# Attention scores of both kinds issued alternately, and a new body for the overflow branch

## The chip, the cores and the metric

The kernel runs on one core of a Trainium2 chip. The metric is the device time of one execution in microseconds; the median of several runs is given. The engines of a core are called PE (TensorE, the matrix engine; PEld are its weight loads), DVE (VectorE), ACT (ScalarE), POOL (GpSimd) and SP (SyncE). Each has its own queue of instructions and waits on semaphores for the others.

## The reference

The input is x of 16 sequences of 256 tokens with 256 features. With xn = layernorm(x), the result is x + attention(xn) + experts(xn).

```python
qkv = einsum('bsd,ed->bse', xn, w_qkv) + b_qkv          # 16 heads of 16
q, k = rotated q and k
scores = einsum('bhqd,bhkd->bhqk', q, k) / sqrt(16)      # causal
attn = softmax(scores); out = einsum('bhqk,bhkd->bhqd', attn, v)

probs = softmax(xn @ router_w.T)                         # 8 experts
w = probs, kept up to a cumulated share of 0.9, else 0
out = sum over e of (silu(xn @ gate_w[e].T) * (xn @ up_w[e].T)) @ down_w[e].T * w[:, e]
```

There are 4096 tokens. An expert works only on the tokens whose weight for it is not zero. Everything is float32.

## The kernel before

**Attention.** A sequence is worked in 8 steps (b, c, p): c is one of 4 chunks of four heads and p one half of a chunk, so a step is two heads (j = 0, 1). Each head's 16 features are padded to 32 rows of the array; a step uses rows 64p to 64p+63. Two kinds of score products exist. `scores` (line 531, tile `s`) has queries on the partitions: a product of 128 columns for the first 128 queries (line 537) and one of 256 for the others (line 543), for both heads. After them `maxima` (line 549) adds the causal mask by a bf16 product (line 552), and DVE takes the row maxima (line 558). When all 8 steps of a sequence are through, `turn` (line 564) adds the negative maxima to the queries as a further feature. `probabilities` (line 577, tile `st`) then computes the same scores with keys on the partitions: 256 columns (line 583), 128 columns (line 589), the mask (line 595), and ACT takes the exponential (line 600). `weigh` multiplies by the values (line 610), `finish` turns the result and adds it to x.

A loop over 128 steps (line 675) issues, in each turn, the scores of step i, the probabilities of step i - 11 (`LAG`, an odd number, so the two kinds use different halves of the array's rows), the maxima of step i, and pieces of the next sequence's preparation and of the router. Each `s` and each `st` tile takes two PSUM banks, one a head, from a pool of three (`ps_sc`, line 239). A scheduler lays out the queue of each engine; in it the four products of s stand ahead of the four of st, or, in some steps, the 128-column pair of s stands ahead of other work and the 256-column pair just ahead of st.

**Experts.** Each expert has room for 1472 tokens (`CAP`) in 12 blocks, and one expert with too many may use one block more. POOL gathers the tokens' rows by indirect DMA (line 362), PE multiplies (lines 755 and 796), and POOL adds the weighted result into the output by an indirect DMA (`contract`, line 802).

**The overflow branch.** If more tokens are without a slot, a flag (`overflow`, read at line 851) sends all engines into a branch (line 854) that goes over all experts: it places the tokens past the slots block by block, gathers their rows, computes and scatters. With these inputs the flag is 0 and the branch is not taken. Its instructions are part of the program, and the engines jump past them; on the way round, the DMA semaphores are raised to the values which they would have after the branch, so that the waits at the end of the program (shown as line 925) hold for both ways.

Of the kernel before, what the change touches and what calls it, by code (L numbers as in the profile page):

```python
# [30 lines left out]
def kernel(  # L31
# [356 lines left out]
    with tc.tile_pool(name="prep", bufs=2) as prep, tc.tile_pool(  # L388
# [139 lines left out]

        W = 3 * P

        def scores(b, c, p):

            qT, kT, _, _ = seqs[b]
            sc = ps_sc.tile([P, 2, 512], F32, tag="sc", name=f"s_{b}_{c}_{p}")
            for j in range(2):
                rows = slice(32 * (2 * p + j), 32 * (2 * p + j) + 32)
                nc.tensor.matmul(  # L537
                    sc[:, j, :P], qT[rows, c, :P], kT[rows, c, :P],
                    start=True, stop=False, skip_group_check=True,
                )  # L540
            for j in range(2):
                rows = slice(32 * (2 * p + j), 32 * (2 * p + j) + 32)
                nc.tensor.matmul(  # L543
                    sc[:, j, P:W], qT[rows, c, P:], kT[rows, c, :],
                    start=False, stop=False, skip_group_check=True,
                )
            return sc

        def maxima(b, c, p, sc):
            for j in range(2):  # L550
                for k in (0, 2):
                    nc.tensor.matmul(  # L552
                        sc[:, j, ts(k, P)], ident_h, mask_h,
                        start=False, stop=True, skip_group_check=True,
                    )
            for qi in range(NQ):
                lo, hi = (0, P) if qi == 0 else (P, W)
                ins = nc.vector.tensor_reduce(  # L558
                    top[b % 2][:, qi, 2 * p : 2 * p + 2, HD + c], sc[:, :, lo:hi],
                    AX.X, ALU.max, negate=True,  # L560
                )
            return ins
# [11 lines left out]
            for c in range(CH):  # L574
                nc.gpsimd.tensor_tensor(qT[:, c, :], qT[:, c, :], topT, ALU.add)  # L575

        def probabilities(b, c, p):

            qT, kT, _, _ = seqs[b]
            sc = ps_sc.tile([P, 2, 512], F32, tag="sc", name=f"st_{b}_{c}_{p}")  # L580
            for j in range(2):
                rows = slice(32 * (2 * p + j), 32 * (2 * p + j) + 32)
                nc.tensor.matmul(  # L583
                    sc[:, j, : 2 * P], kT[rows, c, :P], qT[rows, c, :],
                    start=True, stop=False, skip_group_check=True,
                )
            for j in range(2):
                rows = slice(32 * (2 * p + j), 32 * (2 * p + j) + 32)
                nc.tensor.matmul(
                    sc[:, j, 2 * P : W], kT[rows, c, P:], qT[rows, c, P:],  # L590
                    start=False, stop=False, skip_group_check=True,
                )
            for j in range(2):
                for k in (0, 2):
                    nc.tensor.matmul(  # L595
                        sc[:, j, ts(k, P)], ident_h, maskT_h,
                        start=False, stop=True, skip_group_check=True,
                    )
            pr = probs.tile([P, 2, W], F32, tag="pr", name=f"pr_{b}_{c}_{p}", bufs=6)
            nc.scalar.activation(pr, sc[:, :, :W], AF.Exp)  # L600
            return pr
# [73 lines left out]
        for i in range(len(steps) + LAG + 5):  # L675
            if i < len(steps):
                b, c, p = steps[i]
                if i % PPS == 0 and b + 1 < B:
                    if b > 0:
                        open_seq(b + 1)  # L680
                    jobs = prep_seq(b + 1, turns_only=b == 0)
                sc = scores(b, c, p)
            if 0 <= i - LAG < len(steps):
                k = i - LAG
                prs[k] = probabilities(*steps[k])
            if i < len(steps):
                behind = maxima(b, c, p, sc)
                if jobs is not None:
                    job = next(jobs, None)
                    if job is not None:  # L690
                        job()
                with tc.issue_after(behind.ins):
                    if stat_next < NT:
                        sums_of(stat_next)
                        stat_next += 1
                    if i in stat_jobs:
                        statistics(*stat_jobs[i])

                if i == 2 * PPS + PPS // 2:
                    with tc.issue_after(stored[3].ins):  # L700
                        load_expert(0)
                if i == 3 * PPS:
                    with tc.issue_after(sums[4 * NQ - 1].ins):
                        zero_fill()


                if i % PPS == 5 and b % 2 == 0 and b + 1 < B:
                    parts = router(b * NQ, 2 * NQ)
                    todo = [lambda parts=parts: next(parts, None)] * 6
                    if b + 2 == B:  # L710
                        todo += [
                            lambda: count(0),
                            lambda: find_wave(0, 0),
                            lambda: fetched.update({0: fetch(*work[0])}),
                            lambda: find_wave(0, 1),
                            lambda: fetched.update({1: fetch(*work[1])}),
                        ]
                for _ in range(1 if b + 2 < B else 2):
                    if todo:
                        todo.pop(0)()  # L720
            k = i - 1
            if 0 <= k < len(steps) and k % PPS == PPS - 1:
                turn(steps[k][0])
            k = i - LAG - 2
            if 0 <= k < len(steps) and k % 2 == 1:
                held[k] = weigh(steps[k][0], steps[k][1], (prs.pop(k - 1), prs.pop(k)))
            k = i - LAG - 3
            if 0 <= k < len(steps) and k % 2 == 1:
                finish(steps[k][0], steps[k][1], held.pop(k))


    with tc.tile_pool(name="hid", bufs=2) as hid:
# [55 lines left out]

        added = {}

        def contract(e, k, hT, xg, token, n, name, alone=False):

            _, _, d_sb = expert_w[e]
            py = ps_m.tile([P, D], F32, tag="m", name=f"py_{name}_{k}")
            for i in range(IC):
                nc.tensor.matmul(  # L796
                    py[:n, :], hT[:, i, k * P : k * P + n], d_sb[:, i, :],
                    start=(i == 0), stop=(i == IC - 1),
                )
            ys = hid.tile([P, D], F32, tag="ys", name=f"ys_{name}_{k}", bufs=6)  # L800
            nc.scalar.activation(ys[:n, :], py[:n, :], AF.Copy, scale=weights_of(e, xg, n))  # L801
            ins = nc.gpsimd.indirect_dma_start(  # L802
                out=out, out_offset=bass.IndirectOffsetOnAxis(ap=token, axis=0),
                in_=ys[:n, :], in_offset=None, compute_op=ALU.add,
            )

            if not alone:
                for other in added.setdefault(e, []):
                    tc.declare_no_dep(ins.ins, other, reason="no token in common")
                added[e].append(ins.ins)  # L810

        xT, hT = {}, {}

# [38 lines left out]
            overflow, min_val=0, max_val=1, skip_runtime_bounds_check_because="0 or 1"  # L852
        )
        with tc.If(many > 0):
            upper = gat.tile([P, P], F32, tag="upper", name="upper", bufs=1)
            own = gat.tile([P, 1], F32, tag="own", name="own", bufs=1)
            more = gat.tile([P, P], F32, tag="more", name="more", bufs=1)
            four = gat.tile([P, 4, 1], I32, tag="four", name="four", bufs=1)
            for e in range(E):
                load_expert(e)  # L860
                nc.vector.tensor_scalar(upper, slot[:, :P], float(CAP), None, ALU.add)
                nc.vector.tensor_scalar(own, mine[:, 0:1], float(CAP), None, ALU.add)
                with tc.For_i(0, -(-(NT * P - CAP) // P), 1):
                    place_slots(e // 4, upper, more)
                    nc.vector.tensor_scalar(upper, upper, float(P), None, ALU.add)
                    find(e // 4, (0,), more, own, four, f"o{e}")
                    nc.vector.tensor_scalar(own, own, float(P), None, ALU.add)
                    token = four[:, e % 4, :]
                    xg = fetch_block(token, f"o{e}")
                    xo = open_in(f"o{e}")  # L870
                    turn_in(xo, 0, xg, f"o{e}")
                    ho = open_hidden(f"o{e}")
                    for q in range(IC):
                        expand(e, q, xo, ho, P, f"o{e}")
                    contract(e, 0, ho, xg, token, P, f"o{e}", alone=True)


# [51 lines left out]
```

## Time and profile before

| what | value |
|---|---|
| median of 3 runs | 1006.89 us (1004.35, 1006.89, 1007.24) |
| profiled execution | 1005.13 us, of which the span from first to last instruction is 1002.9 us |
| mean granted clock of TensorE | 0.983 |
| 40 to 440 us (attention) | PE busy 380.6 of 400 us |
| 440 to 520 us (its end, the first experts) | PE busy 78.4 of 80 us |
| 520 to 985 us (experts) | PE busy 463.9 of 465 us |
| 985 to 1003 us (end) | PE busy 0.5 of 18 us |

Busy times of PE are modelled and the products are pipelined, so a busy PE does not mean that it works at its peak; a wait shorter than a product's length can hide in it. The page of the profile gives engine shares and the costliest lines; the timeline gives single instructions in order of time; a query by source line also lists sequencer instructions (waits, branches, drains), marked by a q behind the engine's name (POOLq, SPq).

### The profile page before, as it was taken

The numbers are of one execution on the slowest core, as the hardware profiler recorded it, in microseconds if no ns is written. First come the engines' busy times: TensorE is split into PE (matmuls) and PEld (weight loads), VectorE is DVE, ScalarE is ACT, GpSimd is POOL, SyncE is SP. The second block draws the span as 40 slices with busy tenths as digits, with TensorE's granted clock in tenths as the row PEclk, the third lists the DMA queues.
The fourth block names the chain that finished last, engine by engine and source line by source line (L and its number), as shares of the span: only waits on it lengthen the run. The fifth ranks groups of instructions, "written<-read, shape, count | busy, mean of one in ns | idle before, by whom it ended". The sixth has DMA issues, their size and how long they took to land. (4 is left out here: it accounts for less than half of the span.)

```text
span 1002.9 us, 17633 instructions
## 1 busy us (share of the span) xinstructions
PE 955.6 (95%) x7076; PEld 666.2 (66%) x7076; DVE 428.2 (43%) x1268; ACT 316.7 (32%) x617; POOL 393.5 (39%) x473
## 2 busy tenths in 40 slices
PE   7999999999999999899999999999999999999993
PEld 3576667676767676675676666766766667666672
DVE  6777665757575756725111234332211111111210
ACT  3444644443444344252222221212222222222220
POOL 6324223232222222423455454444444545547332
PEclk9899999999999999899999999999999999999997
DMA  7124100000020000101243343242432524324221
GB/s 237 29 80 151 38 23 23 18 23 24 22 86 23 2 23 2 37 30 53 43 89 69 50 93 62 43 111 43 96 70 44 115 49 96 65 48 98 40 27 22
DMA packets 46362, 57.54 MB, mean 57 GB/s; under 512 B 9312, under 2 KB 37600, under 8 KB 46272
## 3 DMA queue, kind: packets, MB, share of 16 engines
q0 software_dynamic: 19360, 29.81, 16.7%
q1 hardware_dynamic: 26912, 26.52, 8.4%
q8 instruction: 58, 0.95, 0.4%
q14 instruction: 32, 0.26, 0.1%
HBM read 32.14 MB, written 24.17 MB: 56 GB/s over the span
## 5 line engine op out<-in xcount | busy, mean ns | idle before, releaser
L802 POOL DMA_INDIRECT out<-ys,tokens x96 | 152.0, 1583 | 239.6 <-ACT ys L801 186.3
L761 DVE TENSOR_TENSOR hT<-act,gu 128x384 f32<-128x384 f32 (+2 forms) x132 | 70.0, 530 | 333.2 <-ACT act L760 328.5
L755 PE MATMUL gu<-xT,wg 128*128 128x384 f32 (+1 forms) x512 | 182.7, 479 | 1.4 <-DVE hT L761 1.0
L796 PE MATMUL py<-wd,hT 128*128 128x256 f32 (+1 forms) x768 | 182.4, 380 | 0.0
L755 PE MATMUL gu<-xT,wu 128*128 128x384 f32 (+1 forms) x512 | 179.5, 473 | 0.0
L558 DVE TENSOR_REDUCE top<-s 128x2 f32<-128x256 f32 (+1 forms) x256 | 131.0, 552 | 100.3 <-PE s L552 100.3
L796 PEld LDWEIGHTS py<-wd,hT 128*128 128x128 f32 (+1 forms) x768 | 141.5, 186 | 41.7 <-issue 3.8
L760 ACT ACTIVATE act<-gu 128x384 f32<-128x384 f32 (+2 forms) x132 | 62.3, 472 | 285.0 <-PE gu L755 280.5
L600 ACT ACTIVATE pr<-st 128x768 f32<-128x768 f32 x128 | 103.7, 810 | 127.1 <-PE st L595 121.6
L755 PEld LDWEIGHTS gu<-xT,wu 128*128 128x128 f32 x512 | 97.6, 191 | 61.5 <-issue 0.9
L755 PEld LDWEIGHTS gu<-xT,wg 128*128 128x128 f32 x512 | 89.8, 191 | 40.9 <-DVE hT L761 2.7
L362 POOL DMA_INDIRECT xg<-rows,tokens x96 | 94.6, 985 | 40.3 <-issue 20.7
L583 PE MATMUL st<-qT,kT 32*128 32x256 f32 x512 | 90.7, 430 | 1.8 <-DVE less L328 1.0
L631 POOL TENSOR_TENSOR xs<-xs,at 128x128 f32<-128x128 f32 x64 | 29.2, 456 | 145.2 <-DVE at L627 144.7
L801 ACT ACTIVATE ys<-py,xg 128x256 f32<-128x256 f32 x96 | 45.5, 474 | 120.9 <-PE py L796 114.7
L543 PE MATMUL s<-kT,qT 32*128 32x256 f32 x512 | 81.9, 391 | 1.0
L467 POOL TENSOR_TENSOR qp<-qk,rot 128x256 f32<-128x256 f32 x32 | 23.3, 729 | 121.9 <-DVE qk L466 121.9
L610 PE MATMUL o<-pr,va 128*32 128x256 f32 (+1 forms) x1024 | 56.8, 336 | 13.7 <-DVE at L627 11.6
L439 PE MATMUL pq<-wqkv_sb,xnT 128*128 128x512 f32 x128 | 65.4, 635 | 0.2
L537 PE MATMUL s<-kT,qT 32*128 32x128 f32 x512 | 63.4, 322 | 1.1 <-DVE top L558 0.8
L575 POOL TENSOR_TENSOR qT<-qT,topT 128x256 f32<-128x256 f32 x64 | 45.2, 738 | 41.0 <-ACT topT L573 41.0
L537 PEld LDWEIGHTS s<-kT,qT 32*128 32x128 f32 x512 | 39.0, 184 | 23.8 <-issue 21.2
(161 smaller groups left out, 1140.2 us busy)
## 6 DMA issues: line engine op xcount, KB each, us to landing
rows<-xn SPq DMA_DIRECT2D x32, 128.0 KB, 1.8
wg<-in_wg SPq DMA_DIRECT2D x8, 512.0 KB, 3.7
wu<-in_wu SPq DMA_DIRECT2D x8, 512.0 KB, 4.7
wd<-in_wd SPq DMA_DIRECT2D x8, 512.0 KB
out<-xs SPq DMA_DIRECT2D x16, 256.0 KB, 2.1
xs<-in_x SPq DMA_DIRECT2D x3, 1024.0 KB, 9.5
rows<-zeros POOLq DMA_DIRECT2D x1, 1716.0 KB
out<-zeros POOLq DMA_DIRECT2D x1, 1664.0 KB
```

The costliest lines, as they stand in the source:

```text
L362: nc.gpsimd.indirect_dma_start(out=xg[:n, :], out_offset=None, in_=rows, in_offset=bass.IndirectOffsetOnAxis(ap=token, axis=0),)
L439: nc.tensor.matmul(pq, xnT[:, c, ts(qi, P)], wqkv_sb[:, c, : 2 * D], start=(c == 0), stop=(c == DC - 1),)
L537: nc.tensor.matmul(sc[:, j, :P], qT[rows, c, :P], kT[rows, c, :P], start=True, stop=False, skip_group_check=True,)
L543: nc.tensor.matmul(sc[:, j, P:W], qT[rows, c, P:], kT[rows, c, :], start=False, stop=False, skip_group_check=True,)
L558: ins = nc.vector.tensor_reduce(top[b % 2][:, qi, 2 * p : 2 * p + 2, HD + c], sc[:, :, lo:hi], AX.X, ALU.max, negate=True,)
L583: nc.tensor.matmul(sc[:, j, : 2 * P], kT[rows, c, :P], qT[rows, c, :], start=True, stop=False, skip_group_check=True,)
L600: nc.scalar.activation(pr, sc[:, :, :W], AF.Exp)
L755: nc.tensor.matmul(gu[:, j, :w], w_sb[:, c, ts(i, P)], xT[:, c, :w], start=(c == 0), stop=(c == DC - 1),)
L760: nc.scalar.activation(act[:, :w], gu[:, 0, :w], AF.Silu)
L761: nc.vector.tensor_tensor(hT[:, i, :w], act[:, :w], gu[:, 1, :w], ALU.mult)
L796: nc.tensor.matmul(py[:n, :], hT[:, i, k * P : k * P + n], d_sb[:, i, :], start=(i == 0), stop=(i == IC - 1),)
L802: ins = nc.gpsimd.indirect_dma_start(out=out, out_offset=bass.IndirectOffsetOnAxis(ap=token, axis=0), in_=ys[:n, :], in_offset=None, compu ...
```

## The change

`scores` and `probabilities` no longer issue their products. A new function `products` is given the step of the scores and the step of the probabilities, takes a tile for each, and issues first the 128-column pairs of both, then the 256-column pairs of both. For st the 128-column pair is now the one that starts its PSUM bank. The masks, maxima and exponentials follow in the order as before.

The overflow branch gets a new body. It sets the weights of tokens that have a slot to zero, writes the weights back to the table, and then every expert goes over all 32 token tiles with plain DMAs from SP: load the rows, compute, load the output, add on DVE, store. `contract` is split: `product` ends with the weighted result, and `contract` adds the scatter.

```diff
-        def scores(b, c, p):
...
-        def probabilities(b, c, p):
...
+        def products(now, late):
+            made = []
+            for step, by_key in ((now, False), (late, True)):
+                if step is None:
+                    made.append(None)
+                    continue
+                b, c, p = step
+                qT, kT, _, _ = seqs[b]
+                sc = ps_sc.tile(
+                    [P, 2, 512], F32, tag="sc", name=f"{'st' if by_key else 's'}_{b}_{c}_{p}"
                 )
+                made.append((kT if by_key else qT, qT if by_key else kT, c, p, sc, by_key))
+            for first in (True, False):
+                for left, right, c, p, sc, by_key in filter(None, made):
+                    if by_key:
+                        to, lhs = (slice(2 * P, W), slice(P, S)) if first else (
+                            slice(0, 2 * P), slice(0, P))
+                    else:
+                        to, lhs = (slice(0, P),) * 2 if first else (slice(P, W), slice(P, S))
+                    for j in range(2):
+                        rows = slice(32 * (2 * p + j), 32 * (2 * p + j) + 32)
+                        nc.tensor.matmul(
+                            sc[:, j, to], left[rows, c, lhs],
+                            right[rows, c, lhs if first else slice(0, S)],
+                            start=first, stop=False, skip_group_check=True,
+                        )
+            return [m and m[4] for m in made]
...
-                sc = scores(b, c, p)
-            if 0 <= i - LAG < len(steps):
-                k = i - LAG
-                prs[k] = probabilities(*steps[k])
+            k = i - LAG
+            sc, scT = products(
+                steps[i] if i < len(steps) else None,
+                steps[k] if 0 <= k < len(steps) else None,
+            )
+            if scT is not None:
+                prs[k] = probabilities(*steps[k], scT)
...
         with tc.If(many > 0):
-            upper = gat.tile([P, P], F32, tag="upper", name="upper", bufs=1)
...
+            for h in range(NH):
+                place_of = ps_m.tile([P, P], F32, tag="m", name=f"place_{h}")
+                nc.tensor.transpose(place_of, order[h][:, :P], ident)
...
+            nc.sync.dma_start(rt[:, :, D:], wts)
             for e in range(E):
                 load_expert(e)
...
-                    token = four[:, e % 4, :]
-                    xg = fetch_block(token, f"o{e}")
+                with tc.For_i(0, NT, 1) as t:
+                    tile_rows = bass.ts(t, P)
+                    xg = gat.tile([P, D + E], F32, tag="xg", name=f"xg_o{e}")
+                    nc.sync.dma_start(xg, rows[tile_rows, :])
...
-                    contract(e, 0, ho, xg, token, P, f"o{e}", alone=True)
+                    ys = product(e, 0, ho, xg, P, f"o{e}")
+                    had = hid.tile([P, D], F32, tag="had", name=f"had_o{e}", bufs=1)
+                    nc.sync.dma_start(had, out[tile_rows, :])
+                    nc.vector.tensor_tensor(had, had, ys, ALU.add)
+                    nc.sync.dma_start(out[tile_rows, :], had)
```

More of the change, by code (lines that the diff above doesn't have):

```diff
@@ L529 @@
         W = 3 * P
-        def scores(b, c, p):
[L533 to L539, printed above, removed]
-                )
[L541 to L547, printed above, removed]
+        def products(now, late):
[8 more added lines that the diff above has]
+                    [P, 2, 512], F32, tag="sc", name=f"{'st' if by_key else 's'}_{b}_{c}_{p}"
+                )
+                made.append((kT if by_key else qT, qT if by_key else kT, c, p, sc, by_key))
[14 more added lines that the diff above has]
+            return [m and m[4] for m in made]
         def maxima(b, c, p, sc):
@@ L575, in turn, with probabilities @@
                 nc.gpsimd.tensor_tensor(qT[:, c, :], qT[:, c, :], topT, ALU.add)
-        def probabilities(b, c, p):
[L579 to L592, printed above, removed]
+        def probabilities(b, c, p, sc):
             for j in range(2):
@@ L789, with product @@
         added = {}
-        def contract(e, k, hT, xg, token, n, name, alone=False):
+        def product(e, k, hT, xg, n, name):
             _, _, d_sb = expert_w[e]
@@ L801, in contract @@
             nc.scalar.activation(ys[:n, :], py[:n, :], AF.Copy, scale=weights_of(e, xg, n))
+            return ys
+        def contract(e, k, hT, xg, token, n, name):
+            ys = product(e, k, hT, xg, n, name)
             ins = nc.gpsimd.indirect_dma_start(
@@ L805, in contract @@
             )
[L807 to L810, printed above, removed]
+            for other in added.setdefault(e, []):
+                tc.declare_no_dep(ins.ins, other, reason="no token in common")
+            added[e].append(ins.ins)
         xT, hT = {}, {}
@@ L854 @@
         with tc.If(many > 0):
-            upper = gat.tile([P, P], F32, tag="upper", name="upper", bufs=1)
-            own = gat.tile([P, 1], F32, tag="own", name="own", bufs=1)
-            more = gat.tile([P, P], F32, tag="more", name="more", bufs=1)
-            four = gat.tile([P, 4, 1], I32, tag="four", name="four", bufs=1)
+            for h in range(NH):
+                place_of = ps_m.tile([P, P], F32, tag="m", name=f"place_{h}")
+                nc.tensor.transpose(place_of, order[h][:, :P], ident)
+                es = slice(4 * h, 4 * h + 4)
+                nc.vector.scalar_tensor_tensor(
+                    wts[:, :, es].rearrange("p t e -> p e t"),
+                    place_of.rearrange("p (e t) -> p e t", e=4), float(CAP),
+                    wts[:, :, es].rearrange("p t e -> p e t"), ALU.is_gt, ALU.mult,
+                )
+            nc.sync.dma_start(rt[:, :, D:], wts)
             for e in range(E):
                 load_expert(e)
[L861 to L867, printed above, removed]
-                    token = four[:, e % 4, :]
-                    xg = fetch_block(token, f"o{e}")
+                with tc.For_i(0, NT, 1) as t:
+                    tile_rows = bass.ts(t, P)
+                    xg = gat.tile([P, D + E], F32, tag="xg", name=f"xg_o{e}")
+                    nc.sync.dma_start(xg, rows[tile_rows, :])
                     xo = open_in(f"o{e}")
```

## The prediction

> **What bounds the kernel.** I read the page first, then TensorE's timeline around the score products, then the last 20 us by source line.
>
> ```profile
> span 1002.9 us, 17633 instructions
> ...
> PE 955.6 (95%) x7076; PEld 666.2 (66%) x7076; DVE 428.2 (43%) x1268; ACT 316.7 (32%) x617; POOL 393.5 (39%) x473
> ```
>
> TensorE is busy for 95% of the span and every other engine for under half. So a change in the order of TensorE's products counts nearly one for one, and the rest counts only where TensorE has nothing left: at the end. A typical attention step in the timeline of PE (start, length, line, output and inputs, count; an f32 product of two heads shows as two pairs of passes):
>
> ```profile
> 207.74 0.38 PE L537 MATMUL s<-kT,qT 32*128 32x128 f32 x2
> 207.76 0.48 PE L583 MATMUL st<-qT,kT 32*128 32x256 f32 x2
> 207.95 0.28 PE L537 MATMUL s<-kT,qT 32*128 32x128 f32 x2
> 208.06 0.38 PE L543 MATMUL s<-kT,qT 32*128 32x256 f32 x2
> 208.09 0.38 PE L583 MATMUL st<-qT,kT 32*128 32x256 f32 x2
> 208.28 0.38 PE L543 MATMUL s<-kT,qT 32*128 32x256 f32 x2
> 208.30 0.39 PE L589 MATMUL st<-qT,kT 32*128 32x128 f32 x4
> 208.62 0.40 PE L595 MATMUL st<-maskT_h,ident_h 128*128 128x128 bf16 x4
> ```
>
> This is the main finding. In program order all s products stand before st, yet st starts 27 ns after s (unrounded starts), before the second s pass. The two kinds, on different rows of the array, already run side by side. From the first s to the mask product is 0.88 us, and st's own part, 207.76 to 208.62, is what ends last. In other steps st waits for its PSUM tile, and s goes on alone meanwhile:
>
> ```profile
> 320.72 0.38 PE L537 MATMUL s<-kT,qT 32*128 32x128 f32 x2
> 320.80 0.48 PE L583 MATMUL st<-qT,kT 32*128 32x256 f32 x2
> 320.93 0.28 PE L537 MATMUL s<-kT,qT 32*128 32x128 f32 x2
> ...
> 321.66 0.40 PE L595 MATMUL st<-maskT_h,ident_h 128*128 128x128 bf16 x4
> ```
>
> Here st starts 86 ns after s, and again needs 0.854 us to the mask. In a third kind of step other products stand between the 128- and the 256-column s, and the latter starts just ahead of st. The end of the kernel, by source line (engine, operation, count, ns min/median/max, first and last start):
>
> ```profile
> L854 POOLq EVENT_SEMAPHORE  x4: 17/43/1592, 990.6 to 992.4; - x4
> ...
> L854 POOLq COMPARE_BRANCH  x1: 53/53/53, 987.7 to 987.7; - x1
> ...
> L854 POOLq INC_SWDGE_SEM  x1: 2022/2022/2022, 992.5 to 992.5; - x1
> ```
>
> ```profile
> L925 SPq EVENT_SEMAPHORE  x14: 17/28/28, 994.4 to 1002.8; - x14
> L925 POOLq EVENT_SEMAPHORE  x4: 17/17/17, 1002.1 to 1002.8; - x4
> L925 POOLq DRAIN  x3: 50/113/7541, 994.5 to 1002.6; - x3
> ```
>
> The branch is not taken. On its way past it POOL waits for the last scatter to land (the 1592 ns wait, until 992.3), then raises eight DMA semaphores for 2.02 us, and only then begins a drain of 7.54 us (994.5 to 1002.07). The closing barrier takes the last 0.84 us. All of this lies at the end of the span with nothing beside it; that the page's chain of waits stops at 988.9 hides it.
>
> **What the Trainium skill says.** "TensorE: Matmul & The Clock Gate", section The mechanism (packing by rows), says products on different row groups run concurrently, but also that products are in strict order of the program. The trace agrees with the first and not with the second: st passes s products that stand ahead of it. "Runtime: NRT & Kernel Launch", section Instruction fetch mechanics, says a taken branch outside the fetched window waits for its page; POOL's 2.9 us from branch (987.7) to next instruction (990.6) agrees. "VectorE: DVE Perf Modes", section The DRAIN you can't avoid, calls closing drains about 12 ns, constant on all engines; SP, ACT and DVE show 7 to 17 ns here, but POOL shows 7541.
>
> **The change, part by part.** In the compiled order of the two kernels, ahead of the branch DVE, ACT, POOL and SP have the same instructions with the same waits. On TensorE only the score products move: st's 128-column pair goes ahead of s's 256-column pair, and st's 256-column pair comes last. Counts and sizes are equal.
>
> (1) Steps like 207.74. st now has two products ahead of it instead of four; at 27 ns for four it starts about 13 ns after s. Its order becomes 128 then 256, as s has today. s's chain runs from 207.739 to its last pass at 208.282 plus one 256-column pass (213 ns: the two first st starts are 320 apart, less a 107 ns weight load): 756 ns. st's chain is 645 ns to its last start plus a 107 ns pass: 752 ns. So the new st chain should be 4 ns longer, then the same 102 ns until the mask. Net: 13.5 - 4 = 9 ns saved. Sorting all steps by the offset of st to s gives 47 such steps: 0.44 us.
> (2) Steps of the third kind, 27: the 256-column s is no longer ahead of st; 14 ns saved, 4 lost: 0.27 us.
> (3) Steps in which st waits, 43: the wait is for ScalarE's exponential of the step before, and ends when it did. Now s's 256-column pair is queued behind it. Released together with st's, it needs about 550 ns (load plus two passes), under st's 756: hidden. If the passes did not overlap it would cost 2 x 213 ns a step. I take the 4 ns: 0.17 us lost. The 11 steps with st alone lose 0.04 us.
> The sum for TensorE is 0.44 + 0.27 - 0.17 - 0.04 = 0.5 us saved; bounds 0.5 us lost (no gain at the start, 4 ns on all 128) to 1.7 us saved (13.5 ns on all).
>
> (4) The branch's body is not executed in either kernel. But its new body issues no DMA from POOL, and so the way round it changes: the four POOL waits and the raising of semaphores are gone from it; after its jump POOL comes straight to the drain. SP now waits for the last scatter itself, some 0.85 us of waits after 992.3, so until 993.1. POOL's fetch after the branch (2.9 us) stays, so the drain starts at about 990.7 instead of 994.53: 3.85 us earlier. What is late next is the drain itself. Its length without the raising ahead of it is shown nowhere. If it goes with the 204 DMAs that POOL issued (97 gathers, 97 scatters, 8 weight gathers, 2 fills; 7541 / 204 = 37 ns each, my estimate), it is unchanged: the drain ends at 998.2, and 3.85 us are saved. Lower bound of the gain: nothing, if the drain takes over all that was done ahead of it. Upper: 8.9 us, if without the raising it is nearly empty; then SP's waits (993.1) and the 0.84 us barrier close the kernel at 994.0. I take 3.85 because the count of DMAs is the same.
>
> Sum: 0.5 + 3.85 = 4.35 us off the profiled execution of 1005.13 us (span 1002.9, 2.2 outside it): 1000.8 us. The three timed runs (1004.35, 1006.89, 1007.24) lie around it with a median 1.8 higher, so I put the forecast between 1000.8 and 1006.89 - 4.35 = 1002.5: 1001.8 us, which takes 1006.15 as the kernel before. The cases below are counted from there.
>
> **The rivals.** A: the forecast, 1001.8, chance 0.50. 0.3% (3 us) is what a measurement of this kernel can tell from no change, so it counts mostly as faster.
> B: the drain gets short too: 0.5 + 8.9 = 9.4 us saved, 996.7 us. For it: the other drains are 0.05 to 0.18 us, and the long one stands right after the raising. Against: it would have to be caused by an instruction that the profile already charges 2.02 us. Chance 0.15.
> C: the drain waits for the last landing before its work, or takes over half of what was ahead: 992.3 + 7.5 ends at 999.8, so 2.3 + 0.5 = 2.8 us saved or less: 1003.4 to 1004.5. For it: the wait for the landing stood ahead of the drain so far. Against: SP now waits for it too. Chance 0.17.
> D: the end doesn't move, and the TensorE gain of 0.5 us can't be seen: the change does not do what its words say, since the two kinds already ran side by side: 1005.6. For it: nothing in the trace of before tells the drain's length from its end. Chance 0.11.
> E, slower: with st's short pair between s's two pairs, the products no longer pass each other, and s's 256-column load starts only after st's second 128-column pass, 110 ns late, in 117 steps: 12.9 us lost, less 3.85 at the end: 1015.2. It decides from 59 ns a step (117 x 59 = 6.9 us, the 3.85 and 0.3%). Against it: at 207.95 and 208.06 the trace shows s products starting as soon as their own rows are free. Chance 0.07.
>
> **How the numbers follow.** The range may leave out 0.2: it reaches from 996.3 (most of B) to 1006.5 (C, and D with a scatter of 1 us), and leaves out E and the low end of B. Faster by over 0.3%: most of A (0.42), all of B (0.15), a quarter of C (0.04): 0.61. Slower: 0.06 of E and 0.01 of D: 0.07. The rest, 0.32, is the same.
>
> **What would show it.** In the timeline of the changed kernel, st's first pass 13 ns after s, the mask 0.87 us after the first s (0.88 before), and 0.86 after st in steps in which st waits; a mask more than 0.95 after s speaks for E. At the end: no POOLq INC_SWDGE_SEM at the branch, and a long POOLq DRAIN that starts about 3.4 us after the last scatter (987.35 before) and lasts 7.5 us (A), under 2 us (B), or 9 to 11 us (C, D). The prediction is wrong if the drain's end doesn't move, or if SP's waits get late.

## The result

The changed kernel takes 995.04 us (median of 12 runs, 993.16 to 1002.84), the kernel before 1005.14 us (median of 12 runs, 1000.17 to 1010.04). The ratio is 0.9907, with a 95% interval from 0.9881 to 0.9934: faster, by 6.6 to 12 us. The forecast was 1001.8 us with a range down to 996.3. The sign is right; the gain of the medians, 10.1 us, is 2.3 times the 4.35 us forecast, and the time lies outside the range.

The profiled execution of the changed kernel took 994.29 us. Head of its page, as shown for the kernel before:

```profile
span 992.5 us, 17632 instructions
...
PE 946.2 (95%) x7076; PEld 636.7 (64%) x7076; DVE 428.3 (43%) x1268; ACT 316.8 (32%) x617; POOL 393.2 (40%) x473
```

The same number of products and of weight loads; PE is busy for 9.4 us less, while the span is 10.4 us shorter. So most of the gain lies in time in which PE counted as busy. A typical step in PE's timeline of the changed kernel (start, length, line, output and inputs, count):

```profile
399.68 0.38 PE L556 MATMUL s<-kT,qT 32*128 32x128 f32 x2
399.69 0.38 PE L556 MATMUL st<-qT,kT 32*128 32x128 f32 x2
399.89 0.28 PE L556 MATMUL s<-kT,qT 32*128 32x128 f32 x2
399.91 0.28 PE L556 MATMUL st<-qT,kT 32*128 32x128 f32 x2
400.01 0.38 PE L556 MATMUL s<-kT,qT 32*128 32x256 f32 x2
...
400.24 0.38 PE L556 MATMUL st<-qT,kT 32*128 32x256 f32 x2
400.55 0.40 PE L596 MATMUL st<-maskT_h,ident_h 128*128 128x128 bf16 x4
```

st starts 13 ns after s (27 before), the mask stands 870 ns after the first s (881 before). This is what was predicted, and it is small. The gain is elsewhere. One step in eight is the first of a new sequence. PE and then ScalarE around such a step, in the kernel before:

```profile
404.56 0.38 PE L622 MATMUL ot<-ident,oT 128*128 128x128 f32 x2
404.87 0.49 PE L537 MATMUL s<-kT,qT 32*128 32x128 f32 x4
405.43 0.48 PE L543 MATMUL s<-kT,qT 32*128 32x256 f32 x2
405.45 0.48 PE L583 MATMUL st<-qT,kT 32*128 32x256 f32 x2
...
405.98 0.39 PE L589 MATMUL st<-qT,kT 32*128 32x128 f32 x4
406.30 0.40 PE L595 MATMUL st<-maskT_h,ident_h 128*128 128x128 bf16 x4
```

```profile
404.80 0.58 ACT L483 COPY qT<-qt 128x512 f32<-128x512 f32 x1
```

and the same step in the changed kernel:

```profile
401.76 0.38 PE L556 MATMUL s<-kT,qT 32*128 32x128 f32 x2
401.85 0.38 PE L556 MATMUL st<-qT,kT 32*128 32x128 f32 x2
401.98 0.28 PE L556 MATMUL s<-kT,qT 32*128 32x128 f32 x2
402.06 0.28 PE L556 MATMUL st<-qT,kT 32*128 32x128 f32 x2
402.32 0.48 PE L556 MATMUL s<-kT,qT 32*128 32x256 f32 x2
402.34 0.48 PE L556 MATMUL st<-qT,kT 32*128 32x256 f32 x2
...
402.97 0.40 PE L596 MATMUL st<-maskT_h,ident_h 128*128 128x128 bf16 x4
```

```profile
401.69 0.58 ACT L483 COPY qT<-qt 128x512 f32<-128x512 f32 x1
```

The 256-column s needs the second half of the sequence's queries, which ScalarE copies out of PSUM (line 483). In both kernels it starts about 50 ns after the end of that copy (404.80 + 0.58 = 405.38; 401.69 + 0.58 = 402.27); by unrounded times it is 52 or 53 ns in all 14 first steps. Before, the last pass of s's 128-column pair starts at 405.09, and nothing follows on PE until 405.43: all of st is queued behind the waiting s. The products of st themselves could have run: they wait for the exponential of the step before, and in the changed kernel st starts 52 or 53 ns after the end of that exponential in every first step, in the kernel before 541 or 542 ns after it. So afterwards st's 128-column pair runs in this gap, and behind the copy only its 256-column pair is left. From the 256-column s to the mask it takes 868 ns before and 646 ns after. The page shows no idle time here: the modelled lengths of the products (0.49 and more) cover most of the gap.

The end of the changed kernel, by source line:

```profile
L862 POOLq COMPARE_BRANCH  x1: 53/53/53, 980.6 to 980.6; - x1
```

```profile
L939 SPq EVENT_SEMAPHORE  x14: 17/28/29942, 954.4 to 992.4; - x14
L939 POOLq EVENT_SEMAPHORE  x4: 17/17/17, 991.7 to 992.4; - x4
L939 POOLq DRAIN  x3: 50/113/7612, 984.0 to 992.2; - x3
```

From the branch (980.6) POOL comes straight to its drain (984.0); the waits and the raising of semaphores are gone. The drain is about as long as before (7.61 against 7.54 us).

Where the 10.4 us of the two profiled spans lie, from unrounded starts: 0.04 us up to the first mask of st, lost; steps 0 to 109, 3.37 us gained (354.39 to 351.02 us from mask to mask); steps 109 to 127, where the router's work and the first expert begin, 2.64 us (47.26 to 44.62); the experts, until the last scatter, 1.1 us (533.78 to 532.66); from the last scatter to the end 3.3 us (15.56 to 12.25). In the third and fourth of these the clock differs. For the third, two windows show it (the columns are the stretch, its length, busy time and instructions of each engine, then the granted clock, the busy share of the DMA engines and their GB/s):

```profile
404.00:456.00 52.00, 48.82 (x586) 34.76 (x586) 26.33 (x111) 20.95 (x33) 16.70 (x24) 0.90 0.09 28
```

```profile
400.00:450.00 50.00, 46.25 (x604) 29.56 (x600) 26.75 (x111) 21.19 (x34) 16.69 (x24) 0.97 0.11 33
```

The first is of the kernel before, the second of the changed one: 0.90 and 0.97 of full clock. In the fourth, the experts, the clock record of the kernel before has a stretch of 3.4 us at half clock (at 463.1 us), that of the changed kernel none. So these 3.8 us can't be put down to the change from this pair alone.

### The profile page after: what moved, and what is told of

Read it like the earlier page. It is cut to its first block, busy times and chain, and to the rows that moved or that the text cites. A ratio compares the mean times of both kernels' runs of the same rounds, so it can differ in the third digit from the quotient of the medians.

```text
span 992.5 us, 17632 instructions
## 1 busy us (share of the span) xinstructions
PE 946.2 (95%) x7076; PEld 636.7 (64%) x7076; DVE 428.3 (43%) x1268; ACT 316.8 (32%) x617; POOL 393.2 (40%) x473
## 5 line engine op out<-in xcount | busy, mean ns | idle before, releaser
L556 PE MATMUL s<-kT,qT 32*128 32x128 f32 (+1 forms) x1024 | 131.6, 360 | 1.0 <-DVE top L573 0.8
L556 PE MATMUL st<-qT,kT 32*128 32x128 f32 (+1 forms) x1024 | 122.0, 351 | 3.6 <-ACT pr L601 2.0
L556 PEld LDWEIGHTS s<-kT,qT 32*128 32x128 f32 x1024 | 72.3, 185 | 26.3 <-issue 21.0
L556 PEld LDWEIGHTS st<-qT,kT 32*128 32x128 f32 x1024 | 68.1, 185 | 10.9 <-issue 6.7
## 6 DMA issues: line engine op xcount, KB each, us to landing
xs<-in_x SPq DMA_DIRECT2D x3, 1024.0 KB, 11.8
```

Of the source, the lines that this page charges most:

```text
L556: nc.tensor.matmul(sc[:, j, to], left[rows, c, lhs], right[rows, c, lhs if first else slice(0, S)], start=first, stop=False, skip_group_ch ...
```

## The experiments

Two theories. The first: the gain is the gap filled in the 14 first steps, and the earlier drain; the rest of the profiled difference is the clock. The second: the new order is worth something more in steps 109 to 127, or the two halves of the change bring together what neither brings alone. Some runs below measure the end and the gap themselves.

The profiles of all runs, in us. "First step" is the time from the mask before to the mask of a first step; "0 to 107" runs from mask 0 to mask 107 of st and holds 13 first steps; "end" runs from the start of the last scatter to the end of the span.

| kernel | first step | 0 to 107 | end | ratio to before, 95% interval |
|---|---|---|---|---|
| before | 2.64 | 347.18 | 15.56 | |
| the change | 2.42 | 344.06 | 12.25 | 0.9907 [0.9881, 0.9934] |
| new products alone | 2.42 | 344.02 | 15.42 | 0.9961 [0.9943, 0.9980] |
| new branch alone | 2.64 | 347.19 | 11.63 | 0.9954 [0.9936, 0.9972] |
| all but the first steps, new branch | 2.64 | 346.69 | 12.62 | 0.9959 [0.9946, 0.9972] |
| only the first steps, new branch | 2.42 | 344.53 | 11.61 | 0.9934 [0.9910, 0.9959] |
| the change, second time | 2.42 | 344.04 | 12.56 | 0.9904 [0.9883, 0.9925] |
| the change, earlier preparation | 2.15 | 356.36 | 11.85 | 1.0090 [1.0071, 1.0109] |
| before, earlier preparation | 2.15 | 358.05 | 14.89 | 1.0127 [1.0105, 1.0150] |
| the change, more POOL DMAs | 2.42 | 356.96 | 6.61 | one run, 1004.70 us |
| the change, third time | 2.42 | 344.04 | 11.92 | 0.9921 [0.9898, 0.9943] |
| new products alone, second time | 2.42 | 344.02 | 14.80 | 0.9933 [0.9910, 0.9957] |
| new branch alone, second time | 2.64 | 348.30 | 12.01 | 0.9968 [0.9954, 0.9981] |
| the change without the branch | 2.42 | 344.03 | 9.90 | 0.9885 [0.9859, 0.9911] |

**The two halves apart.** New products with the old branch:

> The new order of products with the old overflow branch. Theory 1 (the wait of s's 256-column pair for ScalarE's copy, in one step of eight, is filled by st's 128-column pair: about 220 ns in each of 14 steps, plus about 0.5 us elsewhere): 3.3 us less than before up to step 109, the end of the kernel as before (drain of 7.5 us that starts 7.2 us after the last scatter), ratio 0.9967. Theory 2 (the order of products is worth more, through the stretch around the first dispatch, steps 110 to 116, where the profile of the change gains a further 2.7 us): 6 us less, ratio 0.994.

and old products with the new branch. The helper that issues the products got an argument for the order; False is the order before:

```diff
...
+            if in_turn:
+                for small in (True, False):
+                    for m in filter(None, made):
+                        pair(m, small, small)
+            else:
+                if s:
+                    pair(s, True, True)
+                    pair(s, False, False)
+                if st:
+                    pair(st, False, True)
+                    pair(st, True, False)
...
             sc, scT = products(
                 steps[i] if i < len(steps) else None,
                 steps[k] if 0 <= k < len(steps) else None,
+                False,
             )
```

> The new overflow branch with the old order of products. Theory 1: only the end moves. POOL's drain starts 3.8 us after the start of the last scatter instead of 7.2 and lasts 7.5 to 7.6 us, 3.3 us less, ratio 0.9967; steps 0 to 109 end when they did before, within 0.1 us. Theory 2: the same. If the rest of 2.7 us belongs to the branch (other code positions, other instruction fetches): 6 us less, ratio 0.994.

Measured: 1001.32 us and 1001.04 us against 1005.98. The products alone shorten steps 0 to 107 by 3.16 us and leave the end; the branch alone leaves the steps (347.19) and shortens the end by 3.9 us. Each part moves its own stretch and leaves the other's, as theory 1 has it.

**Which steps.** With the argument `i % PPS != 0` the new order is used in all but the first turn of each sequence:

```diff
...
-                False,
+                i % PPS != 0,
...
```

> As the change, but the first step of each sequence keeps the old order of products. Theory 1: of TensorE's gain only some 0.5 us stays up to step 109; with the end 3.8 us less than before, ratio 0.996. Theory 2: nearly the whole gain stays, 3 us up to step 109, ratio 0.991.

and with `i % PPS == 0` in the first turn alone:

> The new order of products only in the first step of each sequence, with the new branch. Theory 1: 14 steps by 220 ns, 3.1 us less up to step 109, and 3.3 us at the end: ratio 0.9936. Theory 2: 0.2 us up to step 109, and the end: ratio 0.9965.

Measured: 1001.87 and 999.57 us against 1005.98. In steps 0 to 107 the new order in all other steps brings 0.49 us, in the first steps alone 2.65 us; the sum, 3.14, is what the change shows (3.12). So the 13 first steps carry 85% of the gain in the products, 0.2 us each, and the 94 others half a microsecond together, about 5 ns each. (In the first of the two a half-clock stretch at 401.6 us fell between steps 107 and 109; for this reason the table ends at 107.) This settles the place of the gain in steps 0 to 107.

**The gap taken away.** If the wait for the copy is the cause, an earlier copy must remove the gap in either order. One preparation job more in the seventh turn of each sequence brings it one step ahead:

```diff
-                    job = next(jobs, None)
-                    if job is not None:
-                        job()
+                    for _ in range(2 if i % PPS == 6 else 1):
+                        job = next(jobs, None)
+                        if job is not None:
+                            job()
```

> The change, and one preparation job more in turn 6 of each sequence, so that ScalarE's copy of the second half of the queries is done one step before its first use. Theory 1 (first step of each sequence waits for that copy; in the change still about 340 ns of the wait are left: mask 1207 ns after the first s pass instead of 870): that step falls to about 0.87 us, 14 x 0.34 = 4.8 us less up to step 109 than the change (346 instead of 351 us), the whole 4 to 5 us faster than the change on this chip. Theory 2 (these steps are long for another reason, the preparation's own products): they stay at 1.2 us or their work only moves into step 7, and the time is the change's within 1 us.

> The kernel before with the same earlier preparation job, old order of the products, old branch. Theory 1: the stall of 550 ns (1429 instead of 881 from first s to mask) goes without any change of order, 14 x 0.55 = 7.7 us less up to step 109 than before (346.7 instead of 354.4 us), 6 to 8 us faster in the whole; with the copy early the two orders differ by the 11 ns a step only, about 0.5 us, and this kernel and the change with the earlier job differ by the end's 3.3 us plus that. Theory 2: the order itself is worth 3.3 us, and this kernel needs 354 us up to step 109.

Measured: 1014.46 us and 1017.77 us against 1005.76; both kernels got slower, where a gain of 4 to 8 us was expected. In the first step itself the theory held: it takes 2.15 us in most sequences with the one order as with the other, instead of 2.42 and 2.64, and in neither trace does the view of waits list a wait of s for this copy any more. So the wait is the cause of the gap. That both orders take the same 2.15 us doesn't show by itself that the order is worth nothing without the gap, since both stand at a bound that the exponential sets (below); for that the run with all other steps, 5 ns a step, speaks. But the saving is given back, with more. The changed kernel with earlier preparation, PE and then ScalarE:

```profile
276.15 0.61 PE L481 MATMUL kt<-ident,kp 128*128 128x128 f32 x4
276.60 0.60 PE L481 MATMUL qt<-ident,qp 128*128 128x128 f32 x4
277.13 0.48 PE L556 MATMUL s<-kT,qT 32*128 32x128 f32 x2
277.54 0.86 PE L611 MATMUL o<-pr,va 128*32 128x256 f32 x16
278.33 0.37 PE L556 MATMUL s<-kT,qT 32*128 32x128 f32 x1
...
279.97 0.49 PE L556 MATMUL s<-kT,qT 32*128 32x128 f32 x4
280.49 0.38 PE L556 MATMUL st<-qT,kT 32*128 32x128 f32 x2
```

```profile
279.63 0.81 ACT L601 ACTIVATE pr<-st 128x768 f32<-128x768 f32 x1 [0.73 <-PE st L596]
```

The transposes qt now stand in the step before, which is 0.84 us longer or more (2.65 to 3.49 us in this sequence). And the first step is not 0.34 us shorter but 0.27: at 280.49 st starts 50 ns after the end of the exponential of the step before (279.63 + 0.81 = 280.44). The wait for the copy has been replaced by the wait for ScalarE's exponential, and the transposes moved out of the step leave a gap instead of a shorter step; no step from 0 to 107 takes less than 2.15 us in any of the profiles. Three half-clock stretches of 3.4 us, at 90.5, 124.7 and 305.6 us, add about 5 us (an estimate, with 1.7 us for each by the rule that is given below). The expectation had counted the stall alone and not what the moved job brings along.

**The drain.** The forecast took the drain's 7.5 us to go with the number of DMAs that POOL issues. Here the 2 POOL DMAs that fill the padding rows are cut into 52:

```diff
-        nc.gpsimd.dma_start(
-            rows[NT * P :, :].rearrange("(n p) c -> p n c", p=P),
-            zeros.unsqueeze(1).to_broadcast([P, NB, D + E]),
-        )
...
+        for n in range(NB):
+            for h in range(2):
+                r0 = NT * P + n * P + 64 * h
+                nc.gpsimd.dma_start(rows[r0 : r0 + 64, :], zeros[64 * h : 64 * h + 64, :])
+                nc.gpsimd.dma_start(out[r0 : r0 + 64, :], zeros[64 * h : 64 * h + 64, :D])
```

> The change, with the fill of the padding rows by zeros cut from 2 into 48 or more POOL DMAs of half a block (52 in place of 2 if there are 13 blocks), so 254 POOL DMAs instead of 204. If POOL's closing drain goes with the number of DMAs that POOL issued (7612 ns / 204 = 37 ns each), it takes about 9.4 us and the time from last scatter to end grows from 12.3 to 14.1 us. If its length is fixed or goes with the rings alone, it stays at 7.6 us and the end at 12.3 us.

Its end, by source line:

```profile
L859 POOLq COMPARE_BRANCH  x1: 53/53/53, 996.8 to 996.8; - x1
```

```profile
L936 POOLq DRAIN  x3: 50/118/4572, 997.2 to 1002.4; - x3
```

Neither outcome came. With 254 POOL DMAs the drain is shorter, 4.57 us, and the way from the branch to the drain takes 0.43 us instead of 3.4; the end falls to 6.61 us. This drain is recorded from 997.23, while the last scatter is still being issued (until 997.95); from there it takes 3.86 us. Steps 16 and 17, where the fill is issued, lose 12.9 us (a half-clock stretch of 13.7 us lies there too), so the kernel as a whole isn't better (1004.70 us). The rule of 37 ns a DMA is refuted, by one execution; why the drain and the jump got short isn't settled by this run.

In the other kernel the reading of the flag (`values_load`) and the branch are left out:

> The change without reading the flag and without the branch (the handling of tokens past the slots is left out). POOL then runs from its last scatter straight into the drain, with no jump. If the 3.4 us from branch to drain are the fetch of the jump's target alone: the drain starts about 0.4 us after the last scatter instead of 3.8 to 4.1 us, lasts 7.6 us as before, and last scatter to end is 8.9 us instead of 12.3 us. If the drain has to wait for the scatter's landing (about 4.2 us after its start), it gets longer by what it starts earlier, 11 us, and the end stays at 12.3 us. If the drain's 7.6 us are themselves an effect of the jump, as the 4.57 us[...] in the run with more POOL DMAs may say, it falls to 4.6 us or less and the end to 6 us or less.

```profile
L906 POOLq DRAIN  x3: 46/108/9327, 980.6 to 990.5; - x3
```

Measured: 993.40 us; the end takes 9.90 us. The last scatter starts at 980.86 and is issued until 982.41; the drain, recorded from 980.63, ends at 989.96, so 7.55 us after the scatter's issue. Counted so, the drain lasts the 7.5 us without a jump as well: the jump is not its cause. Nor does the landing of the scatter, read from the end of SP's first wait, set its end: the drain ends 7.3 us after it in the changed kernel (984.34 to 991.64) and 5.3 us after it here (984.71 to 989.96). Of the 3.4 us between branch and drain, 2.0 to 2.4 are saved, since the scatter's issue lay beside the jump.

**Do the halves add up?** The first measurements put the change at 0.9907 and the product of its halves, measured on another chip, at 0.9961 x 0.9954 = 0.9915. The change was run again,

> The change itself once more, on the chip of the runs beside it. The change measured alone came out 10.1 us below before, while new products alone and new branch alone give 4.7 + 4.9 = 9.6 us, and at the same mean clock only about 5. Theory 1 (stall of the 256-column s filled in 14 steps, about 3.3 us up to step 109, and 3.3 us at the end, the rest of the profiled 10.4 us being half-clock stretches that fell elsewhere): step 109's mask near 402.97 us less whatever the clock stretches shift, steps 0 to 109 in 351.0 us, last scatter to end 12.3 us, and a median 5 to 7 us below that of before on the same chip when the mean clocks are alike. Theory 2 (products and branch together bring 2 to 4 us more than the sum of both, in the router and first expert stretch): steps 109 to 127 again in 44.6 us instead of 46.8, with the same number of half-clock stretches as before, and a median 9 to 10 us below before.

and then on one chip with both halves:

> The change, this time beside its two halves on one chip. Up to now the change was 9.3 us (median) to 9.7 us below before on two chips, and its halves, measured on a third, 4.7 and 4.9 us; the profiles of the halves account for 3.4 + 3.9 = 7.3 us. Theory 1 (the parts add up, nothing else): on one chip the ratio of the change equals the product of the ratios of its halves within their intervals, and in the profile steps 0 to 109 take 351.0 us and last scatter to end 12.3 us. Theory 2 (the halves together bring 2 to 4 us that neither brings alone): the change's ratio lies 0.002 to 0.004 below the product, and in steps 110 to 116 it again lacks the 1.7 us wait that both halves show in step 114.

> New order of the products, old branch, on the chip of the change beside it. Theory 1: steps 0 to 109 in 351.0 us, last scatter to end 15.4 us, ratio to before 0.9965 (3.4 us). Theory 2: the same here; its step 114 shows the wait of 1.7 us again (3.94 instead of 2.25 us).

> Old order of the products, new branch, on the same chip. Theory 1: steps 0 to 109 in 354.4 us, last scatter to end 11.6 to 12.3 us, ratio to before 0.9963 (3.3 to 3.9 us). Theory 2: the same here; its step 114 shows the wait of 1.7 us again.

Measured: 996.46 us against 1005.76 for the second run; then 997.07, 997.59 and 1002.53 us against 1005.15. On the one chip the product of the halves is 0.9933 x 0.9968 = 0.9901, and the change 0.9921 with an interval that holds it. So there is no sign of more than the sum, within some 2 us either way. Nor does the new order show a gain in steps 109 to 127 when the clock is alike: the old order, in the run with earlier preparation, takes 44.45 us there with one half-clock stretch of 3.4 us, the change 44.62 and 44.66 us with one. The wait of 1.7 us in step 114 shown by both halves on the first chip was in neither here (2.25 and 2.52 us; the latter lies in a half-clock stretch), so it isn't a property of the halves. All four kernels profiled on that chip show it (3.50 to 3.95 us); the kernel before was not profiled there. Steps 0 to 107 repeat to 0.04 us in all runs with the new order whose clock was undisturbed there; the expert stretch takes 532.2 to 532.7 us without a half-clock stretch and 533.5 to 534.3 with one of 3.4 us, for either order. The Trainium skill, "TensorE: Matmul & The Clock Gate", section Terms, puts the penalty of throttled time at about that time multiplied by one minus the ratio of the clock gate. The estimate from it is 1.7 us for 3.4 us at half clock; the traces, with 1.6 us between the two means, agree.

## Why the prediction was partly right

**The base.** The forecast counted from 1006.15 us, the median of 12 runs is 1005.14: 1.0 us of the miss.

**(1), the typical steps: held.** 9 ns a step were predicted, 11 measured. **(3), the steps in which st waits: held.** 4 ns lost were predicted, 3 measured (854 to 857 ns from st to the mask). The run with the new order in all but the first steps shows 0.49 us for them together; the forecast for all of TensorE was 0.5.

**(2), the steps of the third kind: the step that failed.** The prediction said that in 27 steps "other products stand between the 128- and the 256-column s" and gave each 10 ns. That is so in 13 of them, and there it held: 12 of them gain 10 to 15 ns from the first s to the mask, and one loses 0.2 us. In the other 14, the first steps of a sequence, nothing stands between: the 256-column s waits for ScalarE's copy of the queries, and all of st waits with it. The filled gap is 0.22 us a step, 3.1 us instead of 0.14. The prediction sorted the steps by the offset between s and st and priced the difference in position, where it should have asked of each large offset what PE was waiting for. The lines were in the trace: 404.87 and 405.43 for two s pairs that elsewhere follow one another within 0.33 us, and a copy that ends 50 ns before the second. The view of waits of the kernel before even lists the wait, with the weight loads (engine, line, what it waited for, us in total, times, longest):

```profile
PEld s L543 <- ACT qT L483: 3.7, 14, 0.3
```

The 95% busy PE, read as no room for waits, hid it; the Trainium skill, "Perfetto Trace Analysis", section Tensor Engine Instruction (MATMUL, LD_WEIGHTS), says that the end of a product is an estimate and not observed, and here a modelled length of 0.49 us spans most of a gap.

The prediction also held the strict order of products, which the Trainium skill states in "TensorE: Matmul & The Clock Gate", section The mechanism, to be contradicted by the trace. For products that wait on a semaphore the trace agrees with the page: no st queued behind the waiting s passed it in any of the 14 first steps, in either kernel. What ran side by side were products whose inputs were ready.

**(4), the end: held in mechanism, smaller in size.** 3.85 us were predicted. Over the eight profiles with the new branch the end takes 11.6 to 12.6 us (mean 12.06), over the four with the old one 14.8 to 15.6 (mean 15.17): 3.1 us. POOL's drain starts 3.1 to 4.2 us after the last scatter, against 6.4 to 7.2 before. The one profile that the 3.85 us were counted from has the longest end of the four. Rival B, the nearest in time (996.7), is wrong in its cause: the drain kept its length. Its range for the other drains, 0.05 to 0.18 us, is misread as well: POOL's other two take 0.05 and 0.11 us, and the 0.18 us are the clearing of semaphores. C, D and E are excluded by the traces. That the way from the branch to the next instruction is a fetch, as the prediction took it, is not shown by any run.

**The range.** It allowed 1.7 us at most for all of TensorE, from orders and offsets alone; a wait that the order could fill was in neither bound. The gains that the traces fix add to 3.4 + 3.1 = 6.5 us; with step (2) put right, the sum would have given 1005.14 - 6.5 = 998.6 us, still inside the range. The three measurements of the change give 9.4, 9.7 and 7.9 us by their ratios; the interval of the third (5.7 to 10.3) holds 6.5, that of the first (6.6 to 12.0) just misses it and that of the second (7.5 to 11.8) doesn't hold it. So 1.4 to 3.2 us lie outside the two parts.

The mean granted clock of the timed runs says where. On the chip of the second measurement it is 0.9860 for the change and 0.9802 for the kernel before, on that of the third 0.9832 and 0.9801. With half clock as the only lower clock, these are 12 and 6 us less at half clock in an execution, of which the shorter end is 4 us, where nothing is lost. At half a microsecond lost for each that leaves up to 4 and 1 us, my estimate: the size of what is missing. New products alone, with the old end, show a higher clock too (0.9828 against 0.9790, and 0.9850 against 0.9801). So the new order may make half-clock stretches rarer. This is suggested by the clocks and not shown: the branch alone has 0.9824 against 0.9790 on one chip and 0.9812 against 0.9801 on the other, and no run sets the stretches on purpose.

## What to carry to other kernels

A matrix engine that counts as busy can be waiting: compare the starts of equal products over all steps, read the waits of its weight loads, and look for the release in front of every product that comes late. Ready work that stands in a queue behind a wait is a gain to be had: moving a ready pair ahead of the waiting one brought 0.22 us a place, twenty times what the same move brought where nothing waited. Removing the wait instead, by starting its producer earlier, moves the producer's other work too, and the next wait in line (here the exponential) decides what is left. And before a rest of two or three microseconds is explained by the change, compare the granted clocks of the runs.

## What was not expected of the hardware

- POOL's closing drain took 7.54 us in the four profiles with the old branch and 7.61 us in the eight with the new one, all with 204 POOL DMAs, 7.55 us from the last scatter's issue without the branch, and 4.57 us with 254 POOL DMAs.
- The way from POOL's branch, not taken into the body, to its next instruction took 2.7 to 3.7 us in the eight profiles with the new branch (3.4 us in the changed kernel) and 0.43 us in the one with more POOL DMAs.
- Single stretches of 3.4 us at half clock come and go from run to run of the same kernel: the change's stretch from step 109 to 127 took 44.62, 48.28 and 44.66 us in three profiles. In the 14 profiles 33 stretches at half clock begin between the first mask and the last scatter; in the 3.4 us ahead of each of them PE was busy for 36 to 79% of the time. But other windows as idle as that, down to 47%, are followed by full clock, so this alone does not decide.
